# Stationary weights in the routed experts, and results stored by slot instead of scattered by token

## The chip, the core and the metric

The kernel runs on one core of a Trainium2 chip. TensorE (PE) multiplies matrices into PSUM; its weight loads are listed apart as PEld. VectorE (DVE) and ScalarE (ACT) do elementwise work, GpSimd (POOL) does small elementwise work and issues the indirect DMAs, and SyncE (SP) issues most plain DMAs. All data is float32. The metric is the device time of one execution in microseconds; smaller is better. Of the kernel before there are nine timed runs and one profiled execution.

## The reference, cut to what matters

The network works on 1024 tokens (2 x 512) of 256 features and has ten stages in four layers. Four of them are mixture-of-experts blocks: `l0_ffn` runs twice (calls 1 and 2, 32 experts, 6 per token, at most 384 tokens per expert), `l3_ffn` runs twice (calls 3 and 4, 8 experts, 2 per token). Each computes:

```python
scores = router(x)                               # T x E
topk_w, topk_idx = top_k(scores, K)              # normalised to sum 1
xe[e, c] = x[token]                              # slot c of expert e
h  = silu(xe[e] @ w_gate[e]) * (xe[e] @ w_up[e]) # 256 -> 176
ye[e] = h @ w_down[e]                            # 176 -> 256
y[token] = sum over its K experts of topk_w * ye[expert, slot]
out = y + shared_expert(x)
```

Behind call 1 stands the retention layer `l0_attn`. Behind call 2 stands `l1`: a small FFN with binarised weights, sparse attention, and the FFN again, each with a residual and a bias. Behind call 3 stands the state-space mixer `l3_attn`; behind call 4 the output is stored.

## The kernel before, in words

`moe` (L656) is one mixture-of-experts call. It normalises the tokens, computes the router's scores on PE, writes a table with one row per token (256 features and the E expert weights) to HBM, and builds two index lists with `slot_lists` (L440): `get` says for each slot which token to read, `put` says to which row of the tensor `rows` its result goes. `rows` has r rows per token (8 in `l0_ffn`, 2 in `l3_ffn`), one for each of the token's experts. In `l0_ffn` a token can lose an expert to the cap, so `rows` is first filled with zeros (L702, eight POOL DMAs of 768 KB per call). Meanwhile PE runs the shared expert (`shared_unit`, L381).

`experts_sparse` (L533) then runs over units: one unit is one expert with one or two tiles of 128 slots. In `l0_ffn` each of the 32 experts is one unit of two tiles. In `l3_ffn` each of the 8 experts has three tiles, so a unit of two and a unit of one. More slots than that are handled behind a condition (`tc.If`, L728) that asks whether any expert is fuller; the engines read the flag and branch in every run. For a unit:

- `load` (L541): three plain SP DMAs bring the expert's weights into one of five buffers.
- `gather` (L552): one indirect POOL DMA per tile brings 128 rows of the table into `xe`, one of six buffers.
- `turn_x` (L565): PE transposes `xe`, an engine copies it out of PSUM.
- `hidden` (L578): the tokens are the stationary operand, and the gate and up weights (2 x 176 columns) move. ScalarE takes silu, DVE multiplies with up and with the token's weight for this expert.
- `turn_h` (L593): PE transposes h in two halves of 88 features.
- `down_` (L602): four matmuls with h stationary and `w_down` moving, a copy out of PSUM, and one indirect POOL DMA per tile that scatters the rows to `rows` by `put` (L613).

The loop (L639) runs these as a pipeline: in step n it fetches unit n+4, turns x of unit n, turns h of n-2, computes h of n-1 and the result of n-2. The first step is an exception: x of unit 1 is turned behind `hidden` of unit 0.

The sum over a token's experts is left to the stage behind: `add_rows` (L741) is put into `pending`, and that stage calls `settle` for each chunk of 128 tokens. `fetch` (L734) brings `rows` in by plain SP DMAs, chunk by chunk, and `add` (L751) adds them to x, on DVE or with identity matmuls on PE. In `l1` `front` (L1252) settles chunk c and measures it, then `turn_x`, `back`, `measure` and `norm` follow one chunk per step; `scale` (L204) is two small POOL operations. `l1` adds its biases to x on POOL (L1263, L1281). Its attention loop (L1537) projects at L1518.

A planner orders the instructions of each engine in advance, by their place in the program and by when it expects their inputs, except where the kernel writes the order out by hand (`in_order`, L137: in the mixer for PE, ScalarE and DVE, not for POOL). At run time each engine takes its instructions strictly in that order. SP's and POOL's DMAs are issued in the order of these engines too.

## Time and profile before

| What | us |
|---|---|
| median of 9 runs (1925.74 to 1942.36) | 1935.61 |
| profiled execution, its own time | 1937.32 |
| its span | 1935.5 |
| call 1: first x transposed to last result on PE | 66.8 to 230.2 |
| call 2: the same | 468.7 to 631.5 |
| call 3: the same | 1131.7 to 1195.0 |
| call 4: the same | 1850.9 to 1914.1 |
| first fetch of `rows` behind calls 2, 3, 4 | 638.5, 1199.6, 1920.0 |
| `importance` of the second batch in `l1` | 697.0 |

A table like this is read from the order of work of single engines, not from the page alone. The page gives totals over the whole span, and the stages have different limits: PE is busy for 92% of the span, POOL for 47%, but POOL does most of its work inside the four expert loops. DMA shares are means over the core's 16 DMA engines. Where the page says that an engine's idle time was ended "by issue", nothing that the profile shows held it up.

### The profile page before, as it was taken

Reading aid. Unit: us, or ns where it says so; the run is one execution under the profiler, and the core shown is the slowest. Engines: PE = TensorE matmul, PEld = TensorE weight load, DVE = VectorE, ACT = ScalarE, POOL = GpSimd, SP = SyncE. Lnnn points to the kernel's source line nnn. Section 1 sums busy time; section 2 is a strip of 40 time slices with the busy share of each in tenths; the row PEclk is TensorE's granted clock in tenths of the full one; section 3 lists DMA queues with packets and bytes.
Section 4 is the critical chain, followed back from the end, with each engine's and each line's share of the span. In section 5 each row is a group of like instructions: output and inputs, shape, how many; then the busy total and the mean of one; then the engine's idle time right before and its main releaser. Section 6 shows DMA issues by size and latency. Waiting matters only on the chain. (4 is left out here: it accounts for less than half of the span.)

```text
span 1935.5 us, 30397 instructions
## 1 busy us (share of the span) xinstructions
PE 1772.4 (92%) x10906; PEld 1276.7 (66%) x10906; DVE 1151.4 (59%) x2746; ACT 810.9 (42%) x1407; POOL 918.4 (47%) x921
## 2 busy tenths in 40 slices
PE   7999989999999778898889998899999899999995
PEld 5777756666777645544564566577777677777674
DVE  6433286246333476575676553688777777777643
ACT  1132245211333044303651112668787677777221
POOL 3577655423777411200340055056676456767363
PEclk9999999989999989998899998899999999999998
DMA  8375440052654600002120023434545444544133
GB/s 273 116 232 184 158 174 13 12 181 69 191 182 154 215 21 1 23 1 93 54 86 1 23 83 123 138 125 143 174 142 165 130 163 154 162 144 132 46 101 100
DMA packets 117604, 226.54 MB, mean 117 GB/s; under 512 B 22414, under 2 KB 68860, under 8 KB 117302
## 3 DMA queue, kind: packets, MB, share of 16 engines
q1 hardware_dynamic: 88150, 170.17, 27.1%
q0 software_dynamic: 20608, 48.45, 8.0%
q10 hardware_dynamic: 8672, 5.72, 1.0%
q8 instruction: 95, 1.56, 0.3%
q14 instruction: 79, 0.65, 0.1%
HBM read 195.59 MB, written 41.81 MB: 123 GB/s over the span
## 5 line engine op out<-in xcount | busy, mean ns | idle before, releaser
L555 POOL DMA_INDIRECT xe<-table,sl_get x176 | 179.8, 1022 | 190.7 <-DVE sl_get L530 138.2
L583 PE MATMUL ps_gu<-we,xeT 128*128 128x352 f32 x704 | 224.6, 460 | 0.0
L613 POOL DMA_INDIRECT rows<-ye,sl_put x176 | 177.0, 1006 | 71.4 <-issue 38.1
L1869 DVE SCALAR_TENSOR_TENSOR xc<-pp,L_attn_cols,xc 128x511 f32<-128x511 f32 (+2 forms) x216 | 161.4, 747 | 28.7 <-ACT xc L1865 23.4
L608 PE MATMUL ps_ye<-we,hT 88*128 88x256 f32 x704 | 168.1, 379 | 2.9 <-ACT ye L134 1.7
L588 DVE SCALAR_TENSOR_TENSOR he<-se,xe,ps_gu 128x176 f32<-128x176 f32 x176 | 69.9, 397 | 167.4 <-ACT se L587 165.4
L583 PEld LDWEIGHTS ps_gu<-we,xeT 128*128 128x128 f32 x704 | 126.3, 190 | 55.4 <-DVE xeT L132 1.3
L608 PEld LDWEIGHTS ps_ye<-we,hT 88*128 88x128 f32 x704 | 133.2, 190 | 36.7 <-ACT ye L134 3.6
L1976 DVE SCALAR_TENSOR_TENSOR lm<-lm,jb,top 128x128 f32<-128x128 f32 x576 | 153.6, 340 | 0.0
L2085 PE MATMUL yacc<-wt,y 128*128 128x256 f32 x576 | 143.9, 393 | 1.0 <-POOL y L2055 0.7
L2055 POOL TENSOR_TENSOR y<-y,sg 128x512 f32<-128x512 f32 x72 | 91.7, 1273 | 107.0 <-DVE y L2054 105.7
L587 ACT ACTIVATE se<-ps_gu 128x176 f32<-128x176 f32 x176 | 55.8, 317 | 204.9 <-PE ps_gu L583 204.9
L2000 PE MATMUL pz<-xT,wt 128*128 128x128 f32 x1024 | 129.4, 281 | 7.9 <-ACT xt L1949 4.7
L2000 PEld LDWEIGHTS pz<-xT,wt 128*128 128x128 f32 x1024 | 122.7, 196 | 11.0 <-ACT xt L1949 5.7
L1993 POOL TENSOR_TENSOR ce<-ce,CT 128x1024 f32<-128x1024 f32 x54 | 127.9, 2369 | 0.0
L1659 PE MATMUL ps_y<-w8T,xT 128*128 128x512 f32 x256 | 124.0, 618 | 0.0
L1862 PE MATMUL pp<-xT,wx 128*128 128x512 f32 x256 | 122.5, 601 | 1.6 <-DVE jb L1848 0.6
L2085 PEld LDWEIGHTS yacc<-wt,y 128*128 128x128 f32 x576 | 104.4, 191 | 24.3 <-issue 10.4
L2028 PE MATMUL py<-lm,xt 128*64 128x128 f32 x1152 | 109.2, 284 | 12.0 <-ACT xc L1865 4.5
L1985 DVE TENSOR_TENSOR lm<-lm,M 128x1024 f32<-128x1024 f32 x72 | 87.2, 1215 | 47.7 <-ACT lm L1981 45.2
L166 PE MATMUL warm<-cst 128*128 128x256 f32 x340 | 100.5, 437 | 15.7 <-PEq L728 8.6
L2066 POOL TENSOR_TENSOR sqs<-sqs,sq 128x512 f32<-128x512 f32 x56 | 71.4, 1274 | 91.3 <-ACT sq L2065 89.7
(421 smaller groups left out, 3554.2 us busy)
## 6 DMA issues: line engine op xcount, KB each, us to landing
lm<-rows SPq DMA_DIRECT2D x72, 512.0 KB
ce<-rows SPq DMA_DIRECT2D x54, 512.0 KB
rows<-zero POOLq DMA_DIRECT2D x16, 768.0 KB, 13.9
y<-rows SPq DMA_DIRECT2D x16, 768.0 KB
we<-in_L_ffn_w_gate_dram SPq DMA_DIRECT2D x64, 176.0 KB
we<-in_L_ffn_w_up_dram SPq DMA_DIRECT2D x64, 176.0 KB
we<-in_L_ffn_w_down_dram SPq DMA_DIRECT2D x64, 176.0 KB
we<-in_L_ffn_w_dram SPq DMA_DIRECT2D x48, 176.0 KB
```

Of the source, the lines that this page charges most:

```text
L555: nc.gpsimd.indirect_dma_start(xe[:, i, :], None, table, bass.IndirectOffsetOnAxis(get[:, e * per + j : e * per + j + 1], 0), bounds_check ...
L583: nc.tensor.matmul(pg, xeT[:, k, i * P : (i + 1) * P], wgu[:, :, k], start=(k == 0), stop=(k == KD - 1))
L608: nc.tensor.matmul(py[:, i, :], hT[:, q, i * P : (i + 1) * P], wd[:, q, :], start=(q == 0), stop=(q == 1))
L613: put_rows = nc.gpsimd.indirect_dma_start(rows, bass.IndirectOffsetOnAxis(put[:, e * per + j : e * per + j + 1], 0), y[:, i, :], None, bou ...
L1659: nc.tensor.matmul(ps, xT[:, k, :], self.w8T[:, k, 2 * e2 : 2 * e2 + 2, :], start=(k == 0), stop=(k == KD - 1))
L1862: nc.tensor.matmul(pp, wv[:, k, :], xT[:, k, b * S : (b + 1) * S], start=(k == 0), stop=(k == KD - 1))
L1869: nc.vector.scalar_tensor_tensor(out[:, 3 - w :], pp[:, : S - 3 + w], cw[:, m, w : w + 1], out[:, 3 - w :], ALU.mult, ALU.add)
L1976: nc.vector.scalar_tensor_tensor(k["lm"][:, h, :], k["lm"][:, h, :], jb[:, k["c"], n : n + 1], top, ALU.add, ALU.min)
L1993: nc.gpsimd.tensor_tensor(k["ce"], k["ce"], ct, ALU.mult)
L2000: nc.tensor.matmul(pz[:, m, :], u["wz"][:, kk, m * P : (m + 1) * P], xT[:, kk, c * P : (c + 1) * P], start=(kk == 0), stop=(kk == KD - 1),)
L2028: nc.tensor.matmul(py[i * HP : (i + 1) * HP, m, :], w[:, h * HP : (h + 1) * HP], v[:, h, :], start=(m == 0 and n == 0), stop=(n == len(src ...
L2085: nc.tensor.matmul(yacc[cc // 2][:, cc % 2, :], k["y"][:, m, :], u["wo"][:, m, :], start=(u["g"] == 0 and m == 0 and cc % 2 == 0), stop=(u ...
```

## The change

The four expert loops are rewritten, and in calls 2, 3 and 4 (`DENSE`) the way back to the tokens too.

*In all four calls* the weights become the stationary operand: `hidden` gives h already transposed, so `turn_h` goes. The 176 hidden features are split into 112 and 64. The 112 rows of gate and up have a PSUM bank each; the 64 rows of gate and up share one, gate in partitions 0 to 63 and up in 64 to 127. In `down_` the first 112 rows are one matmul per tile, and the 64 rows of tile 0 lie in partitions 0 to 63 and of tile 1 in 64 to 127, with `w_down`'s last 64 rows loaded into both. The token's weight is applied at the end, by ScalarE for tile 0 and by DVE for tile 1. The loop fetches behind `down_` instead of ahead of it, and the exception for unit 1 is gone.

*In calls 2 to 4* `rows` has one row per slot (32 x 384 or 8 x 1024, and a row of zeros in front), and results are stored by a plain SP DMA per unit. `slot_lists` also computes `at`: for each token and rank the row of its result, or 0. The stages behind gather with one indirect POOL DMA per chunk and rank (48 behind call 2, 16 behind calls 3 and 4), for chunk c and c+1 when c is settled. Tiles of `rows` that the main loop doesn't write are zeroed on POOL's queue: one tile of each expert in call 2 (one DMA of 4 MB), five in calls 3 and 4 (five DMAs of 1 MB).

*In `l1`* the biases move from POOL to PE, as a matmul of one row into the same accumulation.

```diff
+DENSE = (2, 3, 4)
...
-    def slot_lists(self, sb, tp, psM, mask, e, n, cap, r):
+    def slot_lists(self, sb, tp, psM, mask, e, n, cap, r, slots, at=None):
...
+        if at is not None:
+            k = at.shape[2]
+            slot = tp.tile([P, e], F32, name="sl_slot")
+            nc.vector.tensor_scalar(slot, self.c["jrow"][:, :e], float(slots), 4097.0, ALU.mult, ALU.add)
+            nc.vector.tensor_tensor(keep, keep, slot.unsqueeze(1).to_broadcast([P, NC, e]), ALU.mult)
+            nc.vector.tensor_tensor(v, v, keep, ALU.add)
+            by = ol.rearrange("p l n -> p (l n)")[:, : k * NC * e].rearrange("p (j n) -> p j n", j=k)
+            for j in range(k):
+                nc.vector.scalar_tensor_tensor(
+                    by[:, j, :], nth.rearrange("p c e -> p (c e)"), float(j + 1), vf, ALU.is_equal, ALU.mult
+                )
+            af = tp.tile([P, k, NC], F32, name="sl_at")
+            nc.vector.tensor_reduce(af, by.rearrange("p j (c e) -> p j c e", e=e), AX.X, ALU.add)
+            nc.vector.tensor_copy(at, af.rearrange("p j c -> p c j"))
...
-            nc.sync.dma_start(wd, down[e].rearrange("(p q) d -> p q d", q=2))
+            nc.sync.dma_start(wd[:H1, 0], down[e][:H1])
+            for i in range(2):
+                nc.sync.dma_start(wd[i * H2 : (i + 1) * H2, 1], down[e][H1:])
...
-        def hidden(n, e, xe, xeT, wgu, nt):
...
-                        pg, xeT[:, k, i * P : (i + 1) * P], wgu[:, :, k], start=(k == 0), stop=(k == KD - 1)
...
-        def turn_h(n, h, nt):
...
+        def hidden(n, xeT, wgu, nt):
+            w = nt * P
+            pg = ps.tile([P, S], F32, name="ps_g")
+            pu = ps.tile([P, S], F32, name="ps_u")
+            pm = ps.tile([P, S], F32, name="ps_m")
+            for i, pt in enumerate((pg, pu)):
+                for k in range(KD):
+                    nc.tensor.matmul(
+                        pt[:H1, :w], wgu[:, i, k, :H1], xeT[:, k, :], start=(k == 0), stop=(k == KD - 1)
+                    )
+            for k in range(KD):
+                for i in range(2):
+                    nc.tensor.matmul(
+                        pm[i * H2 : (i + 1) * H2, :w],
+                        wgu[:, i, k, H1:],
+                        xeT[:, k, :],
...
+            nc.scalar.activation(s1[:H1], pg[:H1, :w], AF.Silu)
+            nc.scalar.activation(s2[H2:], pm[:H2, :w], AF.Silu)
+            nc.vector.tensor_tensor(h1[:H1], s1[:H1], pu[:H1, :w], ALU.mult)
+            for i in range(nt):
+                cs = slice(i * P, (i + 1) * P)
+                nc.vector.tensor_tensor(h2[i * H2 : (i + 1) * H2], s2[H2:, cs], pm[H2:, cs], ALU.mult)
+            return h1, h2
+
+        def down_(n, e, js, xe, hs, wd):
...
+            py = [ps.tile([P, D], F32, name=f"ps_y{'ab'[i]}") for i in range(nt)]
             for i in range(nt):
+                nc.tensor.matmul(py[i], h1[:H1, i * P : (i + 1) * P], wd[:H1, 0, :], start=True, stop=False)
+            for i in range(nt):
+                q = slice(i * H2, (i + 1) * H2)
+                nc.tensor.matmul(py[i], h2[q], wd[q, 1, :], start=False, stop=True)
+            for i in range(nt):
+                scale = xe[:, i, D + e : D + e + 1]
+                if i:
+                    nc.vector.tensor_scalar(y[:, i, :], py[i], scale, None, ALU.mult)
+                else:
+                    nc.scalar.mul(y[:, i, :], py[i], scale)
+            if dense:
+                at = 1 + (e * (rows.shape[0] // P // g.shape[0]) + js[0]) * P
+                nc.sync.dma_start(rows[at : at + nt * P].rearrange("(i p) d -> p i d", p=P), y)
+                return
...
         for n in range(N + 2):
-            if n + ahead < N:
-                fetch(n + ahead)
-            if n < N and n != 1:
+            if n < N and n not in st:
+                fetch(n)
+            if n < N:
                 st[n].append(turn_x(n, st[n][1], len(units[n][1])))
...
+            if n + max(ahead, 1) < N:
+                fetch(n + max(ahead, 1))
...
+                if dense:
+                    nc.scalar.dma_start(rows[0:1], zero[0:1])
+                    sv = rows[1:].rearrange("(e t p) d -> p e t d", e=E, p=P)
+                    with tc.issue_after(normed):
+                        for j in range(len(tiles), slots // P):
+                            nc.gpsimd.dma_start(sv[:, :, j, :], zero.unsqueeze(1).to_broadcast([P, E, D]))
...
+        def gather_rows(c):
+            if c < len(got) or c >= NC:
+                return
+            b, cc = c // CB, c % CB
+            if cc % 2 == 0:
+                fetch(b, cc // 2)
+            for j in range(K):
+                nc.gpsimd.indirect_dma_start(
+                    ys[b, cc // 2][:, cc % 2, j, :],
+                    None,
+                    rows,
+                    bass.IndirectOffsetOnAxis(at[:, c, j : j + 1], 0),
...
         def add_rows(b, cc, psum):
             c, pair = b * CB + cc, cc // 2
+            if dense:
+                gather_rows(c)
+                gather_rows(c + 1)
+                add(b, cc, c, pair, psum)
+                return
...
-                nc.gpsimd.tensor_tensor(self.x[:, c, :], self.x[:, c, :], self.hb, ALU.add)
...
-                    nc.tensor.matmul(ps, xT[:, k, :], self.bwT[:, k, :], start=(k == 0), stop=(k == KD - 1))
+                    nc.tensor.matmul(ps, xT[:, k, :], self.bwT[:, k, :], start=(k == 0), stop=False)
+                nc.tensor.matmul(ps, self.ones[0:1, :], self.hb[0:1, :], start=False, stop=True)
...
-                nc.gpsimd.tensor_tensor(self.x[:, c, :], self.x[:, c, :], bo, ALU.add)
...
-                    nc.tensor.matmul(pw, oT2[:, k, :], wt[:, k, 3, :], start=(k == 0), stop=(k == KD - 1))
+                    nc.tensor.matmul(pw, oT2[:, k, :], wt[:, k, 3, :], start=(k == 0), stop=False)
+                nc.tensor.matmul(pw, self.ones[0:1, :], bo[0:1, :], start=False, stop=True)
```

## The prediction

> **What bounds the kernel now.** I read the page, then busy time by stretch, then the order of work of GpSimd (POOL) and TensorE (PE) in single stretches. The page, with the costliest groups of the routed experts:
>
> ```profile
> span 1935.5 us, 30397 instructions
> ...
> L555 POOL DMA_INDIRECT xe<-table,sl_get x176 | 179.8, 1022 | 190.7 <-DVE sl_get L530 138.2
> L583 PE MATMUL ps_gu<-we,xeT 128*128 128x352 f32 x704 | 224.6, 460 | 0.0
> L613 POOL DMA_INDIRECT rows<-ye,sl_put x176 | 177.0, 1006 | 71.4 <-issue 38.1
> ...
> L608 PE MATMUL ps_ye<-we,hT 88*128 88x256 f32 x704 | 168.1, 379 | 2.9 <-ACT ye L134 1.7
> ```
>
> Busy time by stretch (stretch, length, busy PE, PEld, DVE, ACT, POOL, granted clock, DMA share, GB/s): experts of call 2, the front of l1 behind them, the rest of l1, experts of call 3.
>
> ```profile
> 468.00:635.00 167.00, 163.06 (x780) 127.81 (x779) 61.22 (x119) 48.34 (x112) 126.92 (x126) 1.00 0.55 170
> 635.00:682.00 47.00, 37.48 (x163) 31.20 (x164) 24.24 (x66) 4.48 (x13) 22.66 (x49) 0.91 0.68 234
> 682.00:810.00 128.00, 105.05 (x780) 68.41 (x779) 90.12 (x171) 59.59 (x114) 19.79 (x38) 0.91 0.01 1
> 1131.00:1198.00 67.00, 62.73 (x296) 48.46 (x295) 23.29 (x48) 18.13 (x48) 45.67 (x46) 0.99 0.33 99
> ```
>
> PE is nearly full among the experts, but POOL is as tight. Its order of work (start, duration) there:
>
> ```profile
> 142.53 1.03 POOL L613 DMA_INDIRECT rows<-ye,sl_put  x1 [0.30 <-issue]
> 143.86 1.00 POOL L613 DMA_INDIRECT rows<-ye,sl_put  x1 [0.30 <-issue]
> 145.17 1.03 POOL L555 DMA_INDIRECT xe<-table,sl_get  x1 [0.30 <-issue]
> ```
>
> One indirect DMA each 1.33 us, with nothing between: a unit of two tiles has four, 5.3 us. PE's order of work shows the same unit:
>
> ```profile
> 162.28 0.63 PE L571 MATMUL ps_xe<-cst,xe 128*128 128x128 f32 x4
> 162.74 0.60 PE L597 MATMUL ps_he<-cst,he 128*88 128x128 f32 x4
> 163.18 2.53 PE L583 MATMUL ps_gu<-we,xeT 128*128 128x352 f32 x8
> 165.55 1.89 PE L608 MATMUL ps_ye<-we,hT 88*128 88x256 f32 x8
> ```
>
> From start to start that is 0.46 + 0.44 + 2.37 + 1.73 = 5.00 us. So the two engines are within 7%, and freeing POOL is worth only what PE then gives. A pass over 128 moving columns takes 0.11 us, over 256 columns 0.216 us (1.73/8).
>
> How PE does half-width tiles, from its order of work in the last mixer:
>
> ```profile
> 1413.35 1.95 PE L2000 MATMUL pz<-xT,wt 128*128 128x128 f32 x16
> 1415.23 0.44 PE L2028 MATMUL py<-lm,xt 128*64 128x128 f32 x4
> 1415.50 0.39 PE L2028 MATMUL py<-ce,state 128*64 128x128 f32 x4
> ...
> 1416.81 0.39 PE L2028 MATMUL py<-ce,state 128*64 128x128 f32 x4
> 1417.13 1.99 PE L2085 MATMUL yacc<-wt,y 128*128 128x256 f32 x8
> 1418.96 1.02 PE L2043 MATMUL pst<-xd,Bt 128*128 128x512 f32 x2
> ```
>
> Between 1415.50 and 1416.81 four 64-column passes take 0.218 us: two run at once. But the step into them costs 1.88 - 16 x 0.109 = 0.14 us, and the step out 0.32 - 0.22 at the end and 1.83 - 8 x 0.216 behind it, 0.20 us.
>
> **The change part by part.** Times are against the profiled execution (1937.3 us, span 1935.5), 0.1% above the median of the nine (1935.6).
>
> *PE per unit, all four calls.* Gone: the transposes of h and the 352-column passes. New for two tiles: 4 transposes 0.46; gate and up, 2 x 2 k x 2 passes x 0.216 = 1.73; the middle block, 8 passes in pairs of column halves, 4 x 0.216 = 0.86; down, 4 passes of 112 rows 0.86 and 4 of 64 rows in pairs 0.43. Sum 4.34. Each unit changes the shape of the array four times: into column halves 0.14, out 0.20, into row tiles 0.10 (L1518 to L1456), out into transposes 0.15 (L1456 to L1471): 0.58. So 4.92 us against 5.00. A unit of one tile: 0.22 + 3 x 0.44 + 0.43 + 0.43 + 0.58 = 2.98 against 2.50, since its row tile has no partner.
>
> Here a rule can be weighed. The Trainium skill, TensorEngine Tiling (Array Packing), Theoretical Speedup, promises up to twice the speed for sides of at most 64; the same page's Key Properties warns that changing the tiling mode drains the engine, without a figure. By the first alone a unit is 4.34 us; the rows above show both the pairing and the drain, and give 4.92.
>
> *Call 1* (66 to 234 us). Scatters stay, POOL still issues four per unit: 0, between -2 and +3.
>
> *Call 2.* POOL falls to two gathers, 2.7 us per unit, so PE paces: 32 x 4.92 = 157.4, about 158 with its ends, against 468.7 to 631.5 = 162.8: -5 (with 4.34: -23; if DMA holds the old pace: 0). DMA share 0.55 rises to some 0.66, as the last 64 rows of w_down are loaded twice and stores carry all 256 rows; loads stand four units ahead. SP now issues six DMAs per unit at 0.42, 2.5 us; on its queue a store waits for y, and only a load four units ahead is behind it. ScalarE and DVE have under 2 us per unit each. The fetch of unit n+4 (five loads on SP, two gathers on POOL) moves behind `down_` of n-2: in call 1 its gathers now stand behind that unit's scatters, four units before they are needed, 0; `turn_x(1)` ahead of `hidden(0)` waits for unit 1's gathers (470.2 to some 471.6), 0 to +1.5, taken as the 0.6 of the ends. From PE's end to the first use of rows: 7.0 us before (631.5 to 638.5, scatters lagging PE); now evacuation 0.5 and a plain store 2.6 (a 256 KB fetch, 1919.95 to 1922.58): 3.1, so -4. Together -9.
>
> *The front of l1* pays. 48 gathers x 1.33 = 63.8 us of POOL, none before the last row is stored. Before gather 48 stand some nine `scale` pairs (0.22 + 0.57 with gaps, 0.9): 8.1. Then landing, 3.2 - 1.3 = 1.9, and the chain of the last chunk to the importance of batch 1 (PE adds 2.9, two norms, two transposes, back): 14.5. Sum 88 us; before, 638.5 to 697.0 = 58.4. So +30. In that time batch 0's ranks, compaction, keys and values can run, if they are ordered early; DVE had 5 us of these behind 697, and two score tiles: -6.5. Take +23; bounds +12 (POOL runs all gathers first) and +41 (nothing is hidden, and the work of batch 0 is behind the tail as well). DVE work pulled 40 us ahead in this front before (L1727 at 670) speaks for the lower half. The 16 additions of 0.73 us leave POOL here, and the bias matmuls fall on an idle PE: 0.
>
> *The rest of l1.* 16 bias matmuls of two passes, 0.43 us each, next to a score matmul of the same row tiling: 6.9 us of PE. A period of 10.6 us has 1.5 us of PE waits, which can take 0.86: between 0 and +7, take +4.
>
> *Call 3 and the mixer.* Eight experts x (4.92 + 2.98) = 63.2, before 1131.7 to 1195.0 = 63.3: 0. Rows to first use: 4.6 to 3.1, -1.5. The norms of chunks 0 to 3: five chunks of gathers, 13.3, and three scales stand before the last scale: 17.5 us, against 10.8 (1199.6 to 1210.5): +6.7. Together +5; bounds -5 and +9.
>
> *Call 4 and the end.* Rows 5.9 to 3.1: -2.7. Then 16 x 1.33 = 21.3, landing 1.9, two additions 0.9, the last store 2.9: 27.0, against 15.6 (1919.95 to 1935.5): +11.4. Together +9; bounds -1 and +12.
>
> *Lists and zeros.* Ten DVE operations for `at` (5.5 us in call 2, 1.5 later) fit between sl_get at 463.8 and the first evacuation near 469: 0 to +1.5. Zeros of 5.2 MB more in calls 3 and 4, by five POOL DMAs each: 6.3 MB took 23 us in call 2 (408.6 to 431.8), so 19 us here, 1814 to 1834, before the first gather at 1846.7; 0, and each us beyond that would delay the gathers.
>
> Sum: 0 - 9 + 23 + 4 + 5 + 9 = +32. On the median: 1935.6 + 32 = **1968 us**.
>
> **Rivals.**
> *Shape changes cost nothing among the experts* (a unit is 4.34). For it: dependencies, not the array, may have made part of the steps above. Against: the steps repeat at the same size through the mixer. Call 2 gains 32 x 0.58 = 18.6, calls 3 and 4 16 x 0.58 = 9.3 each: 1968 - 37 = 1931, not slower. It decides from some 4.5 us per unit on down.
> *Nothing of batch 0 is hidden in l1* (its order stays as traced, importance behind the last chunk): +18, 1986. For it: PE took importance(0) only after chunk 7 was turned. Against: L1727 above.
> *The stores do not free PE*: the weight loads or SP's queue hold the old pace. For it: DMA share 0.55 before its bytes grow. Against: the front of l1 ran at 0.68 and 234 GB/s. Price +5, 1973; inside the likeliest one's range.
>
> **How the numbers follow.** Likeliest 0.53 (own range 1950 to 1982), nothing hidden 0.22 (1980 to 2000), free shape changes 0.20 (1910 to 1940), others 0.05. The range 1925 to 1996 leaves out about a tenth at each end. 0.3% (5.8 us) is about what a measurement of this kernel can tell from no change. Faster: most of the third case, 0.17; same 0.05; slower 0.78.
>
> **What would show it.** In the profile after: POOL's two groups of 176 become 176 gathers, 64 scatters and 80 row gathers; units of some 4.9 us in call 2, 5.3 in call 1; PE 0.1 to 0.2 us late at each change of shape; in l1 48 back-to-back DMA_INDIRECT at 1.33 us; a tail of 27 us behind the last store. Wrong if gathers issue faster than 1.3 us, if they start before the last store, or if units are under 4.5 us.

## The result, and the profile after

The changed kernel takes **2046.5 us** (median; 2038.3 to 2054.5) against 1934.2 us for the kernel before: 1.058 times as long, 95% interval 1.056 to 1.060. The direction was forecast; the size was not: +112 us where +32 was written, 50 us above the range.

The page of the changed kernel (line, engine, operation, groups | busy, mean ns | idle before):

```profile
span 2054.1 us, 31945 instructions
...
L573 POOL DMA_INDIRECT xe<-table,sl_get x176 | 177.9, 1011 | 319.9 <-ACT ye L644 116.1
...
L798 POOL DMA_INDIRECT y<-rows,at x80 | 82.2, 1028 | 99.4 <-PEq L775 54.6
```

The 80 row gathers are there, 1.03 us each. Busy time by stretch (the granted clock is the share of TensorE's full speed that the profile shows; stretch, length, busy PE, PEld, DVE, ACT, POOL, granted clock, DMA share, GB/s) for the experts of call 2, the front of l1, the rest of l1, the experts of call 3:

```profile
484.00:652.00 168.00, 165.54 (x901) 105.87 (x899) 61.00 (x150) 48.87 (x112) 60.60 (x61) 1.00 0.65 190
657.00:762.00 105.00, 68.06 (x218) 44.44 (x219) 36.28 (x95) 12.39 (x34) 66.44 (x87) 0.71 0.35 104
772.00:882.00 110.00, 92.69 (x725) 60.91 (x724) 67.89 (x121) 48.24 (x83) 10.21 (x26) 0.89 0.01 1
1210.00:1278.00 68.00, 66.99 (x403) 44.17 (x403) 22.04 (x56) 20.48 (x55) 20.38 (x21) 1.00 0.37 108
```

Among the experts POOL is down to 61 us of 168, as forecast; PE is busier than ever, and the stretch is no shorter. The front of l1 is 105 us, POOL as busy as PE, and PE at a granted clock of 0.71. Where the 118.6 us between the two profiled spans went, by the first and last instruction of each stage in both traces (the profiled execution of the changed kernel took 2056.0 us, 9.5 above the median):

| stage | before | after | more |
|---|---|---|---|
| call 1, start to `sl_get` | 62.3 | 70.1 | 7.8 |
| experts, calls 1 / 2 / 3 / 4 | 163.4 / 162.8 / 63.3 / 63.2 | 167.9 / 167.6 / 68.5 / 68.2 | 4.5 + 4.8 + 5.2 + 5.0 |
| call 2, PE's end to first use of rows | 7.0 | 5.8 | -1.2 |
| front of l1, first use of rows to end of `importance(1)` | 62.3 | 105.3 | 43.0 |
| rest of l1, to the next stage's first `pb` | 124.0 | 139.6 | 15.6 |
| call 3, experts' end to mixer's first `pb` | 41.0 | 54.4 | 13.4 |
| call 4, logits to first transpose | 34.1 | 40.7 | 6.6 |
| call 4, experts' end to the end | 21.4 | 30.3 | 8.9 |
| all other stages | | | 5.0 |

The 6.6 us of call 4's front are mostly one dip of the granted clock: the stretch of the router there shows 0.50, and its logits took 11.8 us in place of 6.7. Call 2's logits met such a dip in both kernels. It does not come with every execution: in a0_after, the changed kernel once more, the logits of calls 2 and 4 took 6.7 us each. So these 6.6 us are not shown to be the change's.

**The unit.** PE's order of work in call 2 (start, duration; a row `128*64` uses 64 of the 128 columns, two of them side by side are the *column halves*; a row `64*128` uses 64 of the 128 rows, two of them are the *row tiles*):

```profile
561.98 0.74 PE L589 MATMUL ps_xe<-cst,xe 128*128 128x128 f32 x4
562.56 1.03 PE L604 MATMUL ps_g<-xeT,we 128*112 128x256 f32 x4
563.42 1.03 PE L604 MATMUL ps_u<-xeT,we 128*112 128x256 f32 x4
564.38 1.08 PE L609 MATMUL ps_m<-xeT,we 128*64 128x256 f32 x8
565.39 0.70 PE L635 MATMUL ps_ya<-we,ha 112*128 112x256 f32 x2
565.93 0.59 PE L635 MATMUL ps_yb<-we,ha 112*128 112x256 f32 x2
566.45 0.48 PE L638 MATMUL ps_ya<-we,hb 64*128 64x256 f32 x1
...
567.09 0.62 PE L589 MATMUL ps_xe<-cst,xe 128*128 128x128 f32 x3
```

5.11 us from start to start. The starts give 0.58, 0.86, 0.96, 1.01, 0.54, 0.52 and 0.64 us; streaming alone would be 0.44, three times 0.86, and three times 0.43. The excess of 0.8 us lies at the changes of shape: 0.10 and 0.15 around the column halves and 0.11 behind them, 0.09 into the row tiles, 0.21 in them, 0.14 out of them.

**The front of l1.** What VectorE waited for there in the changed kernel (us in total, times, longest), and then in the kernel before:

```profile
DVE fxn L215 <- POOL ln_rs L211: 31.8, 8, 9.3
DVE xn L215 <- POOL ln_rsa L211: 17.3, 7, 5.9
DVE y L832 <- DMA y<-rows,at: 14.2, 2, 10.8
```

```profile
DVE xn L214 <- POOL ln_rsa L210: 7.4, 7, 1.1
...
DVE fxn L214 <- POOL ln_rs L210: 5.7, 8, 1.0
```

49 us in all for the chunks' scales against 13. GpSimd's order of work shows one such wait: VectorE had the moments (mean and variance) of chunk 0 at 670.8, and the scale stands behind the gathers of chunks 1 and 2.

```profile
675.58 0.99 POOL L798 DMA_INDIRECT y<-rows,at  x1 [0.30 <-issue]
676.88 1.00 POOL L798 DMA_INDIRECT y<-rows,at  x1 [0.30 <-issue]
677.92 0.26 POOL L210 TENSOR_SCALAR ln_rs<-ln_mv 128x1 f32<-128x1 f32 x1
678.35 1.06 POOL L798 DMA_INDIRECT y<-rows,at  x1 [0.17 <-issue]
679.43 0.60 POOL L211 TENSOR_TENSOR ln_rs<-ln_rs,mhalf 128x1 f32<-128x1 f32 x1
```

When the last rows landed at some 728.4 (issued at 725.6, 2.8 us to landing; 71 us after the first gather), three chunks were still to be done. They come 6.0 and 4.9 us apart, VectorE's additions of their rows:

```profile
728.86 0.41 DVE L829 TENSOR_TENSOR x<-x,ps_add 128x256 f32<-128x256 f32 x1
...
734.84 0.42 DVE L829 TENSOR_TENSOR x<-x,ps_add 128x256 f32<-128x256 f32 x1 [1.07 <-PE ps_add L828]
...
739.69 0.41 DVE L829 TENSOR_TENSOR x<-x,ps_add 128x256 f32<-128x256 f32 x1
```

Then comes the work of batch 0, all of it behind them (`importance(0)` at 744.4); `importance(1)` starts at 759.1 and ends at 762.6.

**The front of call 1** lost 7.8 us in a place that the prediction did not look at. ScalarE's order of work, before and after:

```profile
25.86 1.72 ACTq L695 DMA_DIRECT2D table<-xn  x2
27.61 1.28 ACT L395 ACT_TABLE_LOAD   x1 [1.34 <-issue]
```

```profile
33.10 1.84 ACTq L735 DMA_DIRECT2D table<-xn  x2
34.98 1.28 ACT L396 ACT_TABLE_LOAD   x1 [8.86 <-DMA we<-in_L_ffn_w_down_dram]
```

The program as it was built gives the transfers of SyncE's and ScalarE's queues eight counters in turn, and a transfer waits for the one that used its counter before. With five transfers per expert in place of three, the store of `table` fell behind a `w_down` of the fourth expert, which SyncE issued only at 22.2 us. The program's order has both under one counter:

```
SyncE    L564 DMACopy we_671<-in_L0_ffn_w_down_dram 112x256 [waits DMAHW2_49]
ScalarE  L735 DMACopy table1_80<-xn0_129 128x4x256 [waits DMAHW2_49]
```

SyncE's own issues had slowed from 0.35 to some 1.3 us by then, with the DMA engines at 0.99 to 1.03. `Silu` stands behind the store on ScalarE, and PE waited 5.7 us for it.

### The profile page after: what moved, and what is told of

The parts are those of the page before. It is cut to its first block, busy times and chain, and to the rows that moved or that the text cites. A ratio compares the mean times of both kernels' runs of the same rounds, so it can differ in the third digit from the quotient of the medians.

```text
span 2054.1 us, 31945 instructions
## 1 busy us (share of the span) xinstructions
PE 1835.6 (89%) x11434; PEld 1249.5 (61%) x11434; DVE 1157.0 (56%) x2853; ACT 818.3 (40%) x1423; POOL 874.3 (43%) x868
## 5 line engine op out<-in xcount | busy, mean ns | idle before, releaser
L798 POOL DMA_INDIRECT y<-rows,at x80 | 82.2, 1028 | 99.4 <-PEq L775 54.6
L167 PE MATMUL warm<-cst 128*128 128x256 f32 x340 | 105.8, 456 | 13.8 <-PEq L775 9.9
L623 DVE TENSOR_TENSOR ha<-sa,ps_u 112x256 f32<-112x256 f32 x96 | 38.3, 399 | 136.0 <-PE ps_u L604 124.9
L626 DVE TENSOR_TENSOR hb<-sb,ps_m 64x128 f32<-64x128 f32 x176 | 51.1, 290 | 88.6 <-ACT sb L622 87.5
L2088 POOL TENSOR_TENSOR xd<-xt,dec 128x512 f32<-128x512 f32 x54 | 56.5, 1046 | 97.3 <-ACT xt L2021 97.3
L609 PE MATMUL ps_m<-xeT,we 128*64 128x256 f32 (+1 forms) x768 | 97.2, 374 | 0.0
L644 ACT ACTIVATE ye<-ps_ya,xe 128x256 f32<-128x256 f32 x96 | 45.5, 474 | 118.3 <-PE ps_yb L638 95.9
L604 PE MATMUL ps_g<-xeT,we 128*112 128x256 f32 (+1 forms) x384 | 92.1, 362 | 0.0
```

Source lines behind the costliest of these rows:

```text
L167: self.nc.tensor.matmul(ps[:, :w], self.ident, self.c["le"][:, :w], start=True, stop=True)
L604: nc.tensor.matmul(pt[:H1, :w], wgu[:, i, k, :H1], xeT[:, k, :], start=(k == 0), stop=(k == KD - 1))
L609: nc.tensor.matmul(pm[i * H2 : (i + 1) * H2, :w], wgu[:, i, k, H1:], xeT[:, k, :], start=(k == 0), stop=(k == KD - 1), skip_group_check=True,)
```

## The experiments

On some chips the kernel before takes 1934 us, on three others it took 2032 to 2036; each comparison below is with the kernel before on its own chip.

**Parts alone** (1933.9 for the kernel before). Stationary weights without the dense way back:

```
-DENSE = (2, 3, 4)
+DENSE = ()
```

> The change without its way back: the experts keep their weights stationary, the biases of L1 are added by TensorE, and every call scatters rows by token as before. Theory 1 (three costs stand side by side, read from the two profiles: the experts of the four calls took 4.5, 4.8, 5.2 and 5.0 us longer, the front of call 1 took 7.8 longer, the 24 bias matmuls of 0.35 to 0.43 us some 5 to 10; the rest is the dense way back): 19.5 + 7.8 + 5 to 10, so about 1967 us (1957 to 1975), ratio 1.017. Theory 2 (the experts were slow in the changed kernel only because of what the dense way back sends beside them, as the prediction's unit of 4.92 us would have it): 1926 to 1945. The front of call 1 should still have get at 70 us from the start of the span, since that call scatters in the changed kernel too.

1978.7 us, ratio 1.0215 (1.016 to 1.027); `get` at 70.0, experts 168.3, 167.6, 68.9 and 68.8 us. That is 44.9 us, 12 more than theory 1 summed, most of it the biases, put at half their price (next but one). Theory 2 is out.

```
-DENSE = (2, 3, 4)
+DENSE = (3, 4)
```

> The changed kernel, but call 2 scatters by token and l1 reads its rows with plain transfers; calls 3 and 4 keep slots and gathers. Theory 1 (the 48 row gathers ahead of l1 cost what the front of l1 lost between the two profiles, 43 us, less 2 to 5 of it that are the bias and the clock): the time falls by 38 to 43 from the 2046.5 of the changed kernel, to 2004 to 2009 us. Theory 2 (half of the front's loss comes from something else, the bias matmuls or the lower clock of 0.69): it falls by 20 to 25, to 2022 to 2026.

2006.4 (1.032 to 1.043): 40.1 us less than the changed kernel. The 48 gathers carry the whole loss of l1's front, which is 65 us here. Against e1, slots and gathers of calls 3 and 4 cost 27.7.

```
 def back(c):                                  # kernel before; the same in project(c)
-    nc.tensor.matmul(ps, xT[:, k, :], self.bwT[:, k, :], start=(k == 0), stop=(k == KD - 1))
+    nc.tensor.matmul(ps, xT[:, k, :], self.bwT[:, k, :], start=(k == 0), stop=False)
+nc.tensor.matmul(ps, self.ones[0:1, :], self.hb[0:1, :], start=False, stop=True)
-nc.gpsimd.tensor_tensor(self.x[:, c, :], self.x[:, c, :], self.hb, ALU.add)
```

> The kernel before with one edit: the 24 additions of the two L1 biases go from GpSimd to TensorE, as one more matmul of one row in each sum. Theory 1: TensorE is 82 to 90 per cent busy in the loops of l1, so most of 24 x 0.35 to 0.43 us is seen: 1934 + 4 to 9, 1938 to 1943 us. Theory 2 (TensorE has gaps enough, and GpSimd was what the chain waited for): 1928 to 1935.

1949.6, ratio 1.0077 (1.0048 to 1.0105): +15.7, more than either theory. PE's groups in the attention loop of this run:

```profile
L1517 PE MATMUL pw<-w,oT 128*128 128x256 f32 x32 | 9.0, 405 | 0.1
...
L1518 PE MATMUL pw<-row_L_attn_bo,cst 1*128 1x256 f32 x16 | 5.6, 426 | 0.0
```

A matmul that reads one row lasts as long as one that reads 128, and a bias is two of them: 2 x 0.35 = 0.70 us each (5.6/16), 24 of them 16.8. The trace has +2.9 in l1's front (8 biases), +5.1 in the score loop (10), +2.6 behind it and +3.8 to the next stage's first `pb` (6), 14.4 in all. So the gaps of the front took about half of its share; in the last piece the granted clock was lower too (815 to 834 us: 0.73, against 0.91 in the kernel before).

Why a bias is dearer than its two passes, PE's order of work in the front shows:

```profile
663.86 1.03 PE L1268 MATMUL ps_y<-bwT,fxT 128*128 128x256 f32 x4
664.82 0.69 PE L1269 MATMUL ps_y<-row_L_ffn_bias,cst 1*128 1x256 f32 x2
665.45 0.44 PE L1279 MATMUL pt_n<-cst,xn 128*128 128x128 f32 x2
```

From start to start the four passes ahead of it take 0.96 us where streaming is 0.86, and the two of the bias 0.63 where it is 0.43. A matmul of one row is a change of shape too, at 0.30 us for the way in and out. The score matmuls of the loop already use 32 rows; there the attention's bias makes such a group 1.21 us in place of 0.63, and the FFN's 0.64 in place of 0.63, in each of the last four periods.

```
 def hidden / turn_h / down_                    # the changed kernel, with these of the kernel before
+if dense:
+    nc.sync.dma_start(rows[at : at + nt * P].rearrange("(i p) d -> p i d", p=P), y)
+    return
```

> The changed kernel with the experts of the kernel before (tokens stationary, products transposed, weight of the token multiplied ahead of the way down), while calls 2 to 4 store by slot and the stages behind gather; biases on TensorE. Theory 1 (costs side by side): 2046.5 less 19.5 of the experts less 7.8 of the front of call 1, about 2019 us (2012 to 2024), and the unit of call 2 back at 5.00 us. Theory 2 (a unit freed of its scatters is faster than before, as the prediction allowed for 4.34 to 4.92): below 2010.

2020.1 (1.039 to 1.049), as theory 1 had it. Call 2's experts take 163.3 us with half of GpSimd's work gone: the old unit gains nothing from the freed engine, since PE's 5.00 us is its limit. The parts add up: 44.9 (e1) + 86.2 (e4) - 15.7 (biases, in both) = 115.4, against the measured 112.6.

**The changes of shape.** The left 64 columns of gate and up are packed side by side by ScalarE, so that one block of 128 replaces the two halves:

```
+wm = ew.tile([P, KD, P], F32, name=f"wm{n % 2}")
+for i in range(2):
+    nc.scalar.copy(wm[:, :, i * H2 : (i + 1) * H2], wgu[:, i, :, H1:])
-for i in range(2):
-    nc.tensor.matmul(pm[i * H2 : (i + 1) * H2, :w], wgu[:, i, k, H1:], xeT[:, k, :], ...)
+nc.tensor.matmul(pm[:, :w], wm[:, k, :], xeT[:, k, :], start=(k == 0), stop=(k == KD - 1))
```

> The kernel of the run e1_stationary (1978.7 us) with one edit: the 64 columns that are left of gate and of up are copied side by side by ScalarE, once a unit, so that one stationary block of 128 columns takes the place of the two column halves; two of the four changes of shape of a unit go (measured in the changed kernel at 0.147 into the halves and 0.200 out of them), the streamed columns stay the same. Theory 1 (a change of shape costs PE what the record shows): 0.35 us less for each of the 32 + 32 + 16 + 16 units, the smaller ones a little less, so 25 to 33 us less, about 1949 us (1944 to 1956). Theory 2 (the halves' records only look late, and the unit is long for other reasons, its evacuations or its rounds of PSUM): 1973 to 1982. If ScalarE's copies, 0.5 to 0.8 us a unit on an engine that is 0.30 busy there, become the bound, it is slower than 1980.

> The edit of the run f1_fused again (stationary weights alone, the 64 left columns of gate and up packed side by side by ScalarE, so that the column halves go), on another chip: on the chip of f1_fused the kernel before itself took 2036 us, and engines stood still there inside the experts for 2 to 5 us at a time with nothing to wait for, so that its unit of 4.75 us between such stops did not show in the time. Theory 1 (the two changes of shape of the halves cost what the record shows): where the kernel before takes 1934 us, 25 to 33 us less than the 1978.7 of e1_stationary, 1946 to 1954, and the unit of call 2 at 4.7 to 4.8 us. Theory 2 (the halves are not what makes the unit long): 1973 to 1982.

Both fell on chips where the kernel before took 2036 and 2032: 2049.2 (ratio 1.0078) and 2045.1 (1.0077). Without the stationary kernel's own time on such a chip they decide nothing. The pair that decides was run on a chip with 1933.8 for the kernel before; it also has the biases on GpSimd, the order at the heads of the calls as before, and the fourth expert's loads on GpSimd's queue, and differs in the halves alone:

> The kernel of h2_best and k2_best with the column halves put back (the middle block again as four passes of 64 columns a group, no copies on ScalarE). Theory 1 (the two changes of shape cost what the record shows): where the kernel before takes 1934 us, 25 to 33 us more than n2_best; where it takes 2035 and the experts of the four calls stand still at times for another reason, 10 to 25 more, since part of the gain falls into such stops. Theory 2 (the halves cost nothing): within 5 us of n2_best.

> The kernel of h2_best once more, beside n1_halves. Where the kernel before takes 1934: 1905 to 1928 us, ratio 0.985 to 0.997, its call 2 at 32 x 4.75 + 2 to 3 = 154 to 156 us against 162.8. Where it takes 2035: ratio 0.992 to 0.997, as twice before.

1959.3 (1.0107 to 1.0178) with the halves, 1938.5 (0.9991 to 1.0037) without: 21 us between the medians, and no difference from the kernel before. PE's order of work without the halves, call 2:

```profile
534.30 0.74 PE L590 MATMUL ps_xe<-cst,xe 128*128 128x128 f32 x4
534.88 1.03 PE L611 MATMUL ps_g<-xeT,we 128*112 128x256 f32 x4
535.74 1.03 PE L611 MATMUL ps_u<-xeT,we 128*112 128x256 f32 x4
536.60 1.03 PE L615 MATMUL ps_m<-xeT,wm 128*128 128x256 f32 x4
537.47 0.60 PE L634 MATMUL ps_ya<-we,ha 112*128 112x256 f32 x2
...
539.06 0.74 PE L590 MATMUL ps_xe<-cst,xe 128*128 128x128 f32 x4
```

4.76 us, 0.35 less than 5.11, and the 0.10, 0.15 and 0.11 around the halves are gone. In calls 3 and 4 the experts fall from 68.3 and 68.2 to 63.1 and 62.6 us, 5.2 and 5.6 over 16 units: 0.33 to 0.35 each, seen in full. In calls 1 and 2 only 1.0 and 3.9 us come through, not 32 x 0.35 = 11. So the traces locate 15.7 of the 21 us; the two profiled executions differ by 11.3 in all, that with the halves being the shortest of its five. GpSimd's order of work in the run without the halves says why calls 1 and 2 gain so little:

```profile
530.61 1.02 POOL L649 DMA_INDIRECT rows<-ye,sl_put  x1 [0.31 <-DMA xe<-table,sl_get]
531.94 1.02 POOL L574 DMA_INDIRECT xe<-table,sl_get  x1 [0.30 <-issue]
533.26 1.02 POOL L649 DMA_INDIRECT rows<-ye,sl_put  x1 [0.31 <-issue]
```

128 of them at 1.33 us are 170 us, and from the first gather to the last scatter it took 170.5 (466.6 to 637.1), as in the kernel before (464.3 to 634.7). A faster unit runs into the scatters. The two halves of the change answer each other here (a store by slot frees GpSimd, a short unit uses it), but the unit as written, at 5.11, was too long to collect. The short unit together with stores by slot was not run.

**The wait in call 1.** First the two equal transfers of `w_down` as one, then the fourth expert of call 1 from GpSimd's queue:

```
-for i in range(2):
-    nc.sync.dma_start(wd[i * H2 : (i + 1) * H2, 1], down[e][H1:])
+nc.sync.dma_start(wd[:, 1], down[e][H1:].unsqueeze(0).to_broadcast([2, H2, D]))
```

> The kernel of the run e1_stationary with one edit: the two equal transfers of the lower 64 rows of w_down become one, so that an expert is loaded with 4 transfers and not 5. Theory 1 (the front of call 1 lost 7.8 us because ScalarE's store of the table waits for the counter that it shares with the eighth transfer before it, which was an expert's w_down that SP could issue only at 22.2 us into its full queue): the store waits for an earlier transfer now; it goes out by 29 us in place of 33.1, and get comes at 63 to 67 us in place of 70.0: 3 to 7 us less, 1972 to 1976. Theory 2 (the bytes of the prefetch in flight hold the store up, whatever counter it has; they stay the same): get at 69 to 71, 1977 to 1981.

2079.0 (1.019 to 1.0245 of 2036.5), a miss: the store now shares its counter with the fourth expert's `w_up`, whose issue took SyncE 10.9 us; it went out at 42.1, and `get` came at 78.7. Why that one issue took so long, where the other loads took 0.3 to 2.9, is not shown; the edit also gives `w_down`'s transfer another form, two copies of 64 rows in one, and no run separates the two.

```
+q = nc.gpsimd if self.calls == 1 and e == 3 and not wp else nc.sync
-nc.sync.dma_start(wgu[:, 0], g[e].rearrange("(p k) f -> p k f", k=KD))      # and the other four
+q.dma_start(wgu[:, 0], g[e].rearrange("(p k) f -> p k f", k=KD))
```

> The kernel of e1_stationary with one edit: in call 1 the five transfers of the fourth expert are issued by GpSimd and not by SyncE. Theory 1 (ScalarE's store of the table stood until 33.1 us because the counter it uses was that of the fourth expert's w_down, eight transfers before it in the hardware queues, issued at 22.2): the store goes out at 26 to 28 us, TensorE no longer waits 5.7 us for ScalarE in the shared expert, and get comes at 62 to 64 us in place of 70.0: 6 to 8 us less, 1971 to 1973 where before takes 1934. Theory 2 (the DMA engines, busy to 1.0 until 40 us, hold the store and all else): get at 69 to 71.

```profile
25.45 1.86 ACTq L736 DMA_DIRECT2D table<-xn  x2
27.34 1.28 ACT L396 ACT_TABLE_LOAD   x1 [1.49 <-issue]
```

The store goes out at once and `get` comes at 62.3: the cause is shown, though the DMA engines are as full. (2044.8 where the kernel before takes 2032.)

**The front of l1.** Half of its gathers:

```
-for j in range(K):                              # in gather_rows
+for j in range(min(K, 3)):
-y, xc, n = ys[b, pair][:, cc % 2], self.x[:, c, :], K
+y, xc, n = ys[b, pair][:, cc % 2], self.x[:, c, :], min(K, 3) if dense else K
```

> The changed kernel with half of the row gathers ahead of l1: the last three of a token's six ranks are left out, gathers and additions both, so 24 gathers in place of 48 there (the stages behind calls 3 and 4 gather as before). Theory 1 (GpSimd's 1.30 us a gather sets the pace of l1's front): 24 x 1.30 = 31 us less in the front, from 105 to about 75 us, and 2046 - 31 = about 2015 us. Theory 2 (the front is held by the chain from one engine to the next, chunk by chunk, with TensorE at a granted clock of 0.69; the gathers only fill it): 10 us less at the most, 2036 or more.

Only the front can be read (2168 us in all: tokens altered by it are routed otherwise, and call 3 ran its branch for further slots): 83.4 us in place of 105.3. With 24 gathers less the last rows land 34 us sooner, but that gives 22, between the theories: five chunks are left then in place of three (47 us to the end of the front in place of 34). What holds the chunks back while the gathers run, this run does not show.

```
-turn_x(c - 1); back(c - 2); measure(c - 3); norm(c - 4)     # each under its condition
+turn_x(c); back(c); measure(c); norm(c)                     # importance(0) at c == CB
```

> The changed kernel with another order of writing in the front of l1: each chunk of tokens goes through all its steps before the next chunk is begun, where it was one step per chunk and four chunks under way, and batch 0's importance and ranks are written after chunk 4. Theory 1 (31 us lie behind the last row gather because a chunk's steps stand behind the waits for the next chunks' rows on VectorE and behind their gathers on GpSimd): from the last gather to importance of batch 1 10 to 18 us in place of 31, so 2046 - 13 to 21 = 2025 to 2033 where before takes 1934. Theory 2 (a chunk's chain from engine to engine is itself longer than the 8 us in which its gathers go out): the front gets longer, 2046 to 2075.

2146.6 (1.050 to 1.063 of 2032), theory 2 with much to spare: the front takes 161.5 us. A chunk's steps one after another are 14.3 us, against 4.9 to 6.0 with four chunks under way.

```
-ms[c] = self.scale(sb, f"{nth}_{c}", c)          # add and power on GpSimd
+ms[c] = (self.scale if nth else self.scale_a)(sb, f"{nth}_{c}", c)   # sqrt on ScalarE, reciprocal on VectorE; the same for f"a_{c}"
```

> The changed kernel, with the two steps of each chunk's scale in the front of l1 (add and power, 0.22 to 0.6 us each, 16 pairs) taken off GpSimd: square root on ScalarE, reciprocal on VectorE. The gathers stay. Theory 1 (a chunk's chain crosses GpSimd twice and waits there behind up to six gathers of 1.30 us at each crossing): the chain runs at its own pace beside the gathers, the last importance comes 10 to 16 us behind the last gather in place of 31, and the front takes 75 to 88 us in place of 105: 17 to 30 us less than the changed kernel on the same chip. Theory 2 (the gathers' own pace and the landing of rows set the front): the last importance still 25 to 31 us behind the last gather, 0 to 6 us less in all (GpSimd saves 16 x 0.85 us at the most).

2084.2 beside 2089.1 for the changed kernel on the same chip (ratios 1.022 to 1.028 and 1.026 to 1.031). Theory 1 fell; of theory 2 the 0 to 6 us less in all came true (4.9, inside the noise), its 25 to 31 us behind the last gather did not. The gathers are 6.5 us sooner done, and the front is 109.4 us against 106.1. VectorE's waits in it:

```profile
DVE x L835 <- remote: 33.9, 2, 30.0
DVE y L838 <- DMA y<-rows,at: 16.0, 2, 11.0
DVE ln_rs L160 <- ACT ln_rs L159: 4.8, 6, 1.8
```

The waits for a scale are gone, and one of 30.0 us has taken their place: the addition of chunk 3, released at 745.2, about when the last gather's rows landed, so that five chunks were left for the end (44 us), as in g1. What releases that addition so late the trace does not name; it stays open.

**The chip.** Both kernels once more, unchanged, on a chip with 2034.6 for the kernel before:

> The kernel before itself, for its stages on this chip. Theory 1 (chips differ in the calls' experts, where tokens are scattered, and in nothing else): if the whole takes about 2035 us, the experts of calls 1 and 2 take 185 to 195 us in place of 163, and l1's front 62 us as before. Theory 2 (the chip is slower all over): every stage is 5 per cent longer. If the whole takes 1934, the stages are those already shown.

> The changed kernel itself, beside the kernel before on the same chip. If the kernel before takes 1934 here: 2046, ratio 1.058. If it takes about 2035: by theory 1 call 2 stores by slot and keeps its 168 us, so that the change gives back some 25 us of the chip's loss there, ratio 1.03 to 1.045, and l1's front stays at 105 us against 62. Theory 2 (the chip is slower all over): ratio 1.058 on any chip.

2032.2 and 2089.1: ratio 1.028 (1.026 to 1.031), half the loss shown above. Busy time by stretch, experts of calls 1 and 2 in the kernel before there, and then experts of call 2 and the front of l1 in the changed one:

```profile
67.00:268.00 201.00, 176.49 (x774) 133.32 (x773) 57.16 (x112) 46.75 (x111) 124.87 (x123) 0.94 0.51 157
508.00:708.00 200.00, 178.61 (x772) 134.99 (x771) 57.97 (x114) 46.86 (x112) 124.49 (x123) 0.93 0.46 139
```

```profile
507.00:675.00 168.00, 165.69 (x900) 106.06 (x901) 60.78 (x150) 48.56 (x112) 60.27 (x60) 1.00 0.64 190
680.00:786.00 106.00, 69.00 (x222) 45.02 (x223) 36.47 (x96) 12.39 (x34) 66.79 (x87) 0.71 0.35 103
```

The kernel before loses 37 us in the experts of each of calls 1 and 2, 11 and 14 in those of calls 3 and 4, and nothing elsewhere: all 98 us of the chip. Call 2 of the changed kernel, without scatters, keeps its 168; its call 1 takes 199. Calls 3 and 4, without scatters as well, still take 73.3 and 71.7 in place of 68.5 and 68.2, so the scatters are most of what such a chip costs and not all of it. There the change saves 32 us in call 2's experts (167.6 against 199.9), and l1's front takes 44 (106.1 against 61.7).

**A version of the parts that pay.** Packed block, biases on GpSimd and the heads of the calls as before (x of unit 1 turned behind `hidden` of unit 0), scatters in all calls. First with the single `w_down` transfer, then with GpSimd loading the fourth expert:

> Stationary weights, with what the runs so far speak against taken out: no way back by slot, the biases of L1 on GpSimd as before, the column halves replaced by one packed block, one transfer for the lower rows of w_down, and the transposes of the second unit behind the first unit's products, as before. By the sums: 1978.7 less 15.7 for the biases, 25 to 33 for the halves, 3 to 7 for the front of call 1, and 4 to 9 for the order at the head of the four calls: 1914 to 1931 us, so faster than the 1934 of before by some 10 us if the theories on the halves and on the counter hold, and 1945 to 1955 if they don't.

> Stationary weights with the packed block of h1_fused, the biases of L1 on GpSimd as before, the second unit's transposes behind the first unit's products as before, and the fourth expert of call 1 loaded from GpSimd's queue, so that ScalarE's store of the table waits for a transfer of the third expert. By the sums, where before takes 1934: 1978.7 less 15.7, 25 to 33, 5 to 9 for the heads of the four calls and 5 to 8 for the front of call 1: 1913 to 1928 us, ratio 0.989 to 0.997. If the biases and the order at the heads do not add to the rest, 1935 to 1945.

> The kernel of h2_best again (stationary weights in one packed block, biases and the order at the head as before, the fourth expert of call 1 on GpSimd's queue, scatters by token everywhere). On the chip where the kernel before took 2032 it took 0.995 of it (0.992 to 0.998). If the kernel before takes 1934 here: unit of calls 1 and 2 at 4.75 us against 5.00, 1905 to 1928 us, ratio 0.985 to 0.997. If it takes about 2035: 0.992 to 0.998 again.

f3: 1.006 of the kernel before (1.003 to 1.009), `get` at 78.0 as in f2. h2: 2022.9, 0.995 (0.992 to 0.998); k2, the same kernel on another chip: 2019.4, 0.994 (0.992 to 0.996); n2 above, on a chip with 1934: 1.001. It beats the kernel before by half a per cent on the chips with 2032 to 2035 and equals it where that takes 1934. The sums forecast 1905 to 1928 there; they left out GpSimd's pace in calls 1 and 2, and the order at the heads of the calls, put at 5 to 9 us, gave next to nothing (166.4 against 168.3 us of experts in call 1, 167.5 against 167.6 in call 2).

## Why the prediction was wrong, step by step

The two profiled spans lie 118.6 us apart where the sum says 32. The 86.6 between them: the front of l1 20.0, call 3 and the mixer 13.6, call 2 up to the first use of its rows 12.6, call 1 12.3, the rest of l1 11.6, call 4 and the end 11.5, all other stages 5.0.

- **PE per unit.** Wrong in size: streaming was right (4.31 against 4.34), the four changes of shape were put at 0.58 and cost 0.8. The steps in the mixer's rows (0.14 in, 0.20 out) came back at the halves as 0.25 and 0.11, 0.36 against 0.34; the row tiles were put at 0.25 and took 0.44, their pairs lasting 0.64 and not 0.43. In n2 a unit of one tile takes 0.63 for its two passes without a partner (1149.70 to 1150.33), so that excess belongs to the change of shape and not to the pairing; and with 0.43 + 0.44 = 0.87 us the row tiles came out no cheaper than the 0.86 that four unpaired passes would stream in (an estimate from 0.216 a pass). So a unit is 5.11, 32 of them 163.5, and the two ends of the stage took 4.1 us where 0.6 stood. Of the call-2 term "-5" came +4.8, and +5.2 and +5.0 in calls 3 and 4 where 0 stood. The Trainium skill, TensorEngine Tiling (Array Packing), Key Properties, warns that a change of the tiling mode drains the engine. n1 against n2 shows 0.35 us a unit for the pair of changes at the halves.
- **Call 1 at 0** failed twice: 4.5 us among the experts, and 7.8 in front of them. The term counted only what GpSimd issues. The two loads more per expert are priced for call 2 alone, as issues of SyncE; that they stand ahead of call 1's first unit, and which other transfer shares their counters, was not looked at (h3 shows it: 70.0 to 62.3). The 4.5 are the longer unit.
- **The front of l1, +23: it was 43.** The gathers were right: 63.8 + 8.1 + 1.9 = 73.8 to the last landing, measured 71.1. The failing term is "the chain of the last chunk", 14.5: three chunks were left, 31 us from the last landing (728.4) to the start of `importance(1)` (759.1). Half of the 16 more passes until the last chunk's rows are added (11.3 us, to 739.7, where the term has 2.9), half behind that (19.4 where it has 11.6), where batch 0's work lies. The -6.5 for hidden work was 0. With -2.7 at the gathers that makes the 20. The second rival, nothing of batch 0 hidden, had that part right and came near in size, 23 + 18 = 41; but it named no chunks left over, so that it came so near is in part luck. That the 48 gathers carry the loss is shown by e2, 40 us. Why three chunks are left is shown in part only: the scales wait behind gathers, but with the scales off GpSimd (k1) the front was no shorter, and a wait of 30.0 us whose end is not explained stood in place of theirs.
- **The biases: "0" in the front and "+4"**, with an upper bound of 7, against 15.7 alone (e3). The term for one bias, two passes in 0.43 us, was 0.70, since the change of shape around it was left out; that score matmuls with few rows stand next to it helped one of the two biases of a period and not the other. And the idle PE of the front did not take its share for nothing: +2.9 there, 11.5 behind. The table's 15.6 for the rest of l1 is 4.1 above that; the same loop took 11.5 more in e2 and 15.6 more in e1, so these 4 us come and go with the execution.
- **Call 3 and the mixer +5: 18.6** (5.2 experts, 13.4 behind). The term that failed is "five chunks of gathers, 13.3, and three scales stand before the last scale". GpSimd's order of work in the changed kernel has the gathers of all eight chunks before that scale, six more:

```profile
1304.65 1.11 POOL L798 DMA_INDIRECT y<-rows,at  x1 [0.18 <-issue]
1305.79 0.25 POOL L210 TENSOR_SCALAR ln_rs<-ln_mv 128x1 f32<-128x1 f32 x1
```

  From the first use of rows to the end of the last scale passed 24.7 us (from 1282.0), where the kernel before has 10.4 (1199.6 to 1210.0): 14.3 more. From there to `pb` it is 25.7 against 26.0.
- **Call 4 and the end +9: 20.5**, of which 5.0 experts and 6.6 the clock of that execution. The way back, 8.9, was forecast at 8.7: from the first row gather to the end 26.5 us against 27.0. Both calls' ways back make 22.3 of the 27.7 us between e1 and e2.
- **Rows to first use.** 5.8, 4.0 and 3.8 us behind calls 2, 3 and 4 where 3.1 stood: the page's row puts the gathers' wait down to the branch (`PEq L775`), which the term left out.
- The first rival, free shape changes, is refuted by n1 and n2; the third, that the stores do not free PE, missed the point: POOL was freed and PE was the limit. The direction followed from the ways back (+23, +5 and +9), whose sign was right; the saving among the experts that was set against them did not come.

## What to carry to other kernels

Two engines within 7% of each other have to be priced together: freeing one pays only if the other's unit falls below it, and here the stores by slot freed GpSimd while TensorE's unit grew from 5.00 to 5.11. A visit to a smaller shape of the array has a price of its own, here 0.3 to 0.44 us, be it for half a block or for a bias of one row; packing pays only above that. Where an engine issues long DMAs in a row, look at which steps of a chain its order puts behind them: the last scale of the mixer stood behind 16 gathers and not 10. Behind the last landing stand as many chunks as the pace left over, so count the backlog and not the last chunk. Adding transfers to a stream of loads moves which of them an unrelated store has to wait for: look at the head of the program too, where nothing of the change seems to happen.

## What the runs showed of the hardware

Chips differ by 5% on this kernel, in the routed experts alone: 200 us in place of 163 in calls 1 and 2 with scatters, 168 on either kind of chip in call 2 without them (but 73.3 and 71.7 in place of 68.5 and 68.2 in calls 3 and 4 without them). In the run f1_fused on such a chip ScalarE stood from 562.3 to 567.5 us though the sum it was to read had been made at 563.3 by the record; what it waited for was not found. A matmul over one row took 426 ns, one over 128 rows 405. Two passes of 256 columns with 64, 32 or 1 rows took 0.63 or 0.64 us up to the next matmul of 128 rows, whether one matmul, two or four had the array side by side, where streaming is 0.43. A DMA issue on SyncE took 0.33 to 0.35 us for most loads of the first 13 us and 1.2 to 1.5 us from 19.5 us on (once 10.9, in f2), with the DMA engines busy to 0.95 in the first 18 us and to 1.03 behind them. The granted clock fell to 0.50 over the logits of call 4 in the profiled execution of the changed kernel (11.8 us), and not in that of a0_after, the same kernel (6.7 us).
